# Query stacks of an attention layer filled by twelve moves inside SBUF instead of by a trip over DRAM

## The chip, the cores and the metric

The kernel runs on one core of a Trainium2 chip, with all data in float32. The metric is the time of one execution on the device in microseconds (us). Given are the median, the lowest and the highest of several runs, and one further execution that the hardware profiler recorded.

## The reference

One layer with two residual parts, for 4 sequences of 512 tokens, 1024 wide: attention with 32 query heads of 32 columns that share one head of keys and values, a bias linear in the distance (ALiBi) and a causal mask; then a linear map whose weights are stored as 6-bit codes.

```python
# x: (4, 512, 1024)
h = layernorm(x)
q = (h @ Wq).reshape(b, s, 32, 32)
k, v = split(h @ Wkv)                       # one head of 32 columns each
scores = einsum('bqhd,bkd->bhqk', q, k) * 32**-0.5
scores = where(causal, scores + slopes * (key_pos - query_pos), -inf)
x = x + einsum('bhqk,bkd->bqhd', softmax(scores), v).reshape(b, s, 1024) @ Wo
w = (unpack(qweight) - weight_zero_point) * weight_scale      # (1024, 1024)
x = x + layernorm(x) @ w.T + bias
```

## The kernel before

Every float32 operand of the large products is split into a high and a low part of the fast matmul type (float32r), and a product is the sum of high by high, high by low and low by high. The helper `split` does this: ScalarE rounds to the high part (L412), VectorE subtracts to get the low one (L415).

**Phase one** runs over 4 sequences times 8 groups of 4 heads, so 32 groups. For each group:

- `queries`: 24 matmuls form q transposed in the PSUM tile `pq` (L682: 128 rows = 4 heads x 32 columns, by 512 tokens). `split` writes `qh` and `ql`, each with a single buffer. From them comes the **stack** `qs` of the group, a tile of 126 rows by 4 heads by 512 tokens, in three buffers. Its rows 0 to 31 and 64 to 95 hold qh, rows 32 to 63 hold ql, always with the head's 32 columns as rows and the four heads side by side; rows 96 to 123 hold the bias rows `qr_d`, and two more rows hold the negated row maxima, high and low. As the heads lie below each other in qh and side by side in the stack, the rows have to change partitions. Before, qh and ql are written to the DRAM scratch `q_d` and three moves read them back, rearranged.
- `maxima`: scores `s` against the stack of keys `kst` (L738: 16 matmuls in 10 PSUM banks, of which two are in use at a time), and VectorE takes each row's maximum under the causal mask (L751, into `junk` and `mx`). A transpose on TensorE (`trm`, L767) turns the maxima; their high and low part `mt` go into the stack's last two rows by two small moves (qs<-mt).
- `attention`: scores again, transposed and with the maximum taken off by the stack's rows (`st`, L819, 11 matmuls). ScalarE takes the exponential into `p` (L829), GpSimd masks it (L838) and adds the parts up for the denominators (L860). The products with v (`pav`, L848) and the denominators (`den`, L877) run tiled, four heads next to each other in the array. The result `a` goes to the DRAM scratch `at_d` (L869).

Beside this, phase one prepares the next weights (`wq`, later `wo`; load, ScalarE high part L487, GpSimd low part L489), normalises and turns the tokens of the next sequence (`tr`, L598; `pkv`, L616), and unpacks the codes to the scratch `wf_d` (L912 to L945).

**Phase two** runs over 16 token tiles: load `at_d` and the inverse denominators (`raw`), product with Wo (`po`, L1047), residual, layer norm, transpose, product with the unpacked weights (`pf`, L1167), scale, bias and zero point, store. `ffn_rows` loads the bias, scale and zero-point rows on GpSimd's DMA queue.

All of this is first recorded as operations with a wanted time `at`, a cost, and what each reads and writes. `Work.order` then lays every operation out by estimated costs and due times, in several rounds forwards and backwards, and writes down the order of every engine. So the order on all queues comes from this planner: an operation whose cost or dependences change can move others far away. The planner counts 450 ns on SyncE's queue for issuing one DMA, then its bytes at a shared rate, and 2000 ns until it has landed. All ordinary moves of a kernel run through `move` (L420), so their profile line is L420 whatever they move; SyncE's queue is one queue in order, and a waiting DMA holds up those behind it.

Of the kernel before, what the change touches and what calls it, by code (L numbers as in the profile page):

```python
# [42 lines left out]
P = 128  # L43
# [298 lines left out]
def layer_kernel(  # L342
# [64 lines left out]
    def dma(at, size, fn, out, ins, eng="SP"):  # L407
        work.op(eng, at, 0.0, fn, out, ins, size=size)
# [13 lines left out]

    qr_d = tc.dram_tile([NG, N_BIAS, GH, S], F32R, name="qr_d")
    at_d = tc.dram_tile([NG, P, B * S], F32, name="at_d")
    q_d = tc.dram_tile([4, 2, P, S], F32R, name="q_d")
    rden_d = tc.dram_tile([B, GH, NG, S], F32, name="rden_d")
    qr_i = [work.item() for _ in range(NG)]
    at_i = [work.item() for _ in range(B)]
    q_i = [[work.item() for _ in range(2)] for _ in range(4)]
    rden_i = [work.item() for _ in range(B)]  # L430


# [242 lines left out]
    def queries(at, i):  # L675
        b, g = divmod(i, NG)
        pq = new("ps_q", "q", [P, S], F32, f"pq_{i}")
        hi, lo = wq[g]
        for c in range(KC):
            def three(c=c):  # L680
                for n, (w, s) in enumerate(((hi, 0), (lo, 0), (hi, 1))):
                    nc.tensor.matmul(  # L682
                        pq(), w()[:, c, :], xc[b, c]()[:, s, :],
                        start=(c == 0 and n == 0), stop=(c == KC - 1 and n == 2),
                    )
            h = c // (KC // 2)
# [6 lines left out]
        qs[i] = [(0, GH, new("qs", "qs", [P, GH, S], F32R, f"qs_{i}"))]  # L693
        for s, src in enumerate((qh, ql)):
            dma(
                at + 0.6 + 0.7 * s, 262e3,
                lambda s=s, src=src: move(q_d[i % 4, s], src()), [q_i[i % 4][s]], [src],
            )
        for h, n, q in qs[i]:
            dma(  # L700
                at + 1.0, 57e3 * n,
                lambda h=h, n=n, q=q: move(q()[R_BIAS:R_MAX, :, :], qr_d[g, :, h : h + n, :]),
                [(q, "b")], [qr_i[g]],
            )
# [12 lines left out]
    def part(i, h):  # L717

        return next((q, h - first) for first, n, q in qs[i] if first <= h < first + n)


    S_BANKS = [((3, h),) for h in range(GH)] + [((2, h), (0, h)) for h in range(GH)]
    S_BANKS += [tuple((1, h) for h in (2 * i, 2 * i + 1)) for i in range(2)]
    ROWS = (0, 1, 2, "b")

    def maxima(at, i):
        b = i // NG
        k = kst[b % 2]
        mx = new("small", "mx", [P, GH * NT], F32, f"mx_{i}")
        for n, bank in enumerate(S_BANKS):  # L730
            ps = new("ps_s", "s", [P, S], F32, f"s_{i}_{n}")
            widths = [(t + 1) * P for t, _ in bank]
            places = [sum(widths[:m]) for m in range(len(bank))]

            def products(ps=ps, bank=bank, widths=widths, places=places):
                for (t, h), W, o in zip(bank, widths, places):
                    q, at = part(i, h)
                    nc.tensor.matmul(  # L738
                        ps()[:, o : o + W], q()[0:R_MAX, at, ts(t, P)], k()[0:R_MAX, :W],
                        start=True, stop=True,  # L740
                    )
            pe(
                at + 1.2 * n, widths, products, [ps],
                [(q, r) for q in {part(i, h)[0] for _, h in bank} for r in ROWS] + [k],
                more=5.0,
            )
            for (t, h), W, o in zip(bank, widths, places):
                junk = new("q1", "junk", [P, S], F32, f"junk_{i}_{t}_{h}")
                dve(
                    at + 1.2 * n + 0.3, W,  # L750
                    lambda ps=ps, junk=junk, t=t, h=h, W=W, o=o: nc.vector.tensor_tensor_reduce(  # L751
                        out=junk()[:, :W],
                        in0=ps()[:, o : o + W],
                        in1=mask()[:, S - W :],
                        scale=1.0,
                        scalar=-3e38,
                        op0=ALU.add,
                        op1=ALU.max,
                        accum_out=mx()[:, h * NT + t : h * NT + t + 1],
                    ),  # L760
                    [(mx, (t, h))], [ps], more=125.0,
                )
        at += 1.2 * len(S_BANKS)
        N = GH * NT
        tr = new("ps_misc", "misc", [P, P], F32, f"trm_{i}")
        pe(
            at, [P], lambda: nc.tensor.transpose(tr()[0:N, :], mx(), ident()), [tr], [mx]  # L767
        )
        for s in range(2):
            m = new("mt", f"mt{s}", [N, P], F32R, f"mt{s}_{i}")  # L770
            if s == 0:
                hi = m
                act(at + 0.2, P, lambda: nc.scalar.copy(hi(), tr()[0:N, :]), [hi], [tr])
            else:
                lo = m
                dve(
                    at + 0.4, P,
                    lambda: nc.vector.tensor_tensor(
                        lo(), tr()[0:N, :], hi().bitcast(F32), ALU.subtract
                    ),  # L780
                    [lo], [tr, hi],
                )
            for h, n, q in qs[i]:
                dma(
                    at + 0.5 + 0.2 * s, 2e3 * n,
                    lambda m=m, s=s, h=h, n=n, q=q: move(
                        q()[R_MAX + s : R_MAX + s + 1, :, :], m()[h * NT : (h + n) * NT, :]
                    ),
                    [(q, f"m{s}")], [m],
                )  # L790


    ST_BANKS = [(0, (h,)) for h in range(GH)] + [(1, (h,)) for h in range(GH)]
# [2 lines left out]

    def attention(at, i):
        b, g = divmod(i, NG)
        k = kst[b % 2]
        pr = {}  # L800
        for j in range(NT):
            W = S - j * P
# [2 lines left out]
        for n, (j, heads) in enumerate(ST_BANKS):  # L805
            W = S - j * P
            ps = new("ps_st", "st", [P, len(heads), W], F32, f"st_{i}_{n}")
            own = slice(heads[0], heads[-1] + 1)
            runs = []
            for first, m, q in qs[i]:  # L810
                lo, hi = max(first, heads[0]), min(first + m, heads[-1] + 1)
                if lo < hi:
                    runs.append((
                        q, slice(lo - first, hi - first), slice(lo - heads[0], hi - heads[0])
                    ))

            def products(ps=ps, j=j, runs=runs):
                for q, mine, place in runs:
                    nc.tensor.matmul(  # L819
                        ps()[:, place, :], k()[0:R_ALL, ts(j, P)], q()[0:R_ALL, mine, j * P :],  # L820
                        start=True, stop=True,
                    )
            pe(
                at + 1.2 * n, [len(heads) * W / len(runs)] * len(runs), products, [ps],
                [q for q, _, _ in runs] + [k], more=5.0,
            )
            act(
                at + 1.2 * n + 0.3, len(heads) * W,
                lambda ps=ps, own=own, j=j: nc.scalar.activation(  # L829
                    pr[j]()[:, own, :], ps(), AF.Exp  # L830
                ),
                [(pr[j], h) for h in heads], [ps],
            )
# [466 lines left out]
```

## Time and profile before

| what | value |
|---|---|
| median of 3 runs (lowest to highest) | 829.49 us (828.11 to 829.87) |
| the profiled execution | 825.42 us |
| its span, first to last instruction | 823.5 us |
| granted TensorE clock, mean | 0.994 |
| VectorE, ScalarE, GpSimd busy | 69%, 45%, 62% |
| DMA | 133.39 MB, 162 GB/s on average, 57% of the 16 DMA engines on the main queue |

The profiled execution spends 825.42 - 823.5 = 1.92 us around its span and lies 4.07 us below the median of the runs. Every duration that is taken from the profile belongs to that execution. PE is the TensorE matmul, PEld its weight load, DVE is VectorE, ACT is ScalarE, POOL is GpSimd, SP is SyncE; a q behind the name (SPq) means that engine's sequencer, which issues the DMAs. In the waits, the numbers are the total in us, how many times, and the longest.

### The profile page before, as it was taken

To read this page: it belongs to the slowest core of one execution; us is meant where nothing else is said; L and a number is where in the kernel's file an instruction comes from. 1 tells how busy PE (TensorE), PEld (TensorE's weight loads), DVE (VectorE), ACT (ScalarE), POOL (GpSimd) and SP (SyncE) were. 2 spreads that over 40 slices of the span, in tenths; PEclk is the share of its full clock that TensorE was granted. 3 is DMA by queue.
4 is the path that set the end of the run, shared out by engine and by line. 5 is a ranking of instruction groups with operands and counts; after the bars stand their busy time and mean duration, and the time that the engine had idled before them with its cause. 6 is when DMAs were issued, how large, how long until landed. Compare 5 with 4: busy or idle time off the path is not lost.

```text
span 823.5 us, 13425 instructions
## 1 busy us (share of the span) xinstructions
PE 795.9 (97%) x4480; PEld 594.7 (72%) x4480; DVE 565.5 (69%) x1491; ACT 372.3 (45%) x659; POOL 514.1 (62%) x442
## 2 busy tenths in 40 slices
PE   5979999999999999999999999999999999999997
PEld 4756676777676767676775767667888888888885
DVE  7476777388786388777367675644998666666865
ACT  4336575464775445675556564330233323332320
POOL 4337977276787375877489896879465445554333
PEclk9989999999999999999999999999999999999999
DMA  7885853395553387543567966526875755665321
GB/s 223 245 252 154 232 164 91 111 266 188 155 145 100 106 262 211 148 120 111 174 174 194 235 189 208 170 58 171 214 178 158 173 131 129 152 151 137 97 52 51
DMA packets 131796, 133.39 MB, mean 162 GB/s; under 512 B 42964, under 2 KB 93140, under 8 KB 130704
## 3 DMA queue, kind: packets, MB, share of 16 engines
q1 hardware_dynamic: 130912, 129.01, 57.0%
q0 software_dynamic: 816, 3.53, 1.7%
q8 instruction: 35, 0.57, 0.3%
q14 instruction: 33, 0.27, 0.1%
HBM read 85.58 MB, written 39.85 MB: 152 GB/s over the span
## 4 chain that ended last, share of the span: by engine, by line
PE 89%; DVE 4%; DMA 2%; ACT 2%; issue 1%; POOL 1%; SPq 1%; DVEq 0%; ACTq 0%; POOLq 0%
PE po L1047 21%; PE pq L682 21%; PE pf L1167 13%; PE st L819 9%; PE s L738 9%; PE pav L848 8%; PE den L877 4%; PE pkv L616 2%; PE tr L598 2%; DVE junk L751 2%; ACT p L829 1%; POOL p L860 1%; DMA wo_st<-in_L_attn_Wo_dram 1%; DMA qs<-mt 1%; SPq L420 1%
## 5 line engine op out<-in xcount | busy, mean ns | idle before, releaser
L751 DVE CUSTOM_DVE_ANT_0 junk<-s,mask 128x384 f32<-128x384 f32 (+3 forms) x512 | 250.6, 490 | 119.6 <-PE s L738 88.8
L860 POOL TENSOR_TENSOR p<-p,p 128x1536 f32<-128x1536 f32 (+2 forms) x96 | 232.4, 2421 | 16.7 <-PE pav L848 15.0
L829 ACT ACTIVATE p<-st 128x512 f32<-128x512 f32 (+1 forms) x352 | 183.9, 559 | 115.8 <-PE st L819 110.7
L682 PE MATMUL pq<-xc,wqh 128*128 128x512 f32 x512 | 198.5, 405 | 2.3 <-DVE ql L415 1.4
L1047 PE MATMUL po<-woh,aT 128*128 128x512 f32 x512 | 164.8, 391 | 0.0
L838 POOL TENSOR_SCALAR_AFFINE_SELECT p<-p 128x512 f32<-128x512 f32 x128 | 82.2, 647 | 105.1 <-ACT p L829 104.3
L738 PE MATMUL s<-kst,qs 124*128 124x384 f32 (+3 forms) x512 | 127.5, 324 | 3.9 <-DVE mx L751 3.6
L819 PE MATMUL st<-qs,kst 126*128 126x512 f32 (+1 forms) x352 | 127.1, 399 | 3.9 <-ACT p L829 2.9
L1167 PE MATMUL pf<-wf,xT 128*128 128x512 f32 x512 | 121.1, 390 | 0.7 <-DVE xT L415 0.7
L738 PEld LDWEIGHTS s<-kst,qs 124*128 124x128 f32 x512 | 91.5, 189 | 34.2 <-DVE mx L751 8.9
L682 PEld LDWEIGHTS pq<-xc,wqh 128*128 128x128 f32 x512 | 97.7, 191 | 23.8 <-issue 2.7
L1047 PEld LDWEIGHTS po<-woh,aT 128*128 128x128 f32 x512 | 96.1, 188 | 21.7 <-DVE mx L751 0.8
L1167 PEld LDWEIGHTS pf<-wf,xT 128*128 128x128 f32 x512 | 95.8, 188 | 20.9 <-DVE xT L415 1.1
L682 PE MATMUL pq<-xc,wql 128*128 128x512 f32 x256 | 101.8, 398 | 0.1
L1047 PE MATMUL po<-wol,aT 128*128 128x512 f32 x256 | 99.7, 389 | 0.0
L819 PEld LDWEIGHTS st<-qs,kst 126*128 126x128 f32 x352 | 63.5, 190 | 25.7 <-ACT p L829 10.8
L848 PE MATMUL pav<-p,kv 128*32 128x512 f32 (+3 forms) x1024 | 79.9, 436 | 0.0
L848 PEld LDWEIGHTS pav<-p,kv 128*32 128x32 f32 x1024 | 29.6, 109 | 48.8 <-issue 37.6
L1187 POOL TENSOR_TENSOR x<-x,y 128x512 f32<-128x512 f32 x30 | 42.7, 1425 | 27.4 <-DVE y L1178 27.4
L1047 PEld LDWEIGHTS po<-wol,aT 128*128 128x128 f32 x256 | 48.1, 188 | 9.6
L538 POOL TENSOR_SCALAR rstd_f<-mv_f 128x1 f32<-128x1 f32 x16 | 3.9, 244 | 81.7 <-DVE mv_f L533 72.7
L682 PEld LDWEIGHTS pq<-xc,wql 128*128 128x128 f32 x256 | 49.2, 192 | 7.2 <-POOL wql L489 0.6
(92 smaller groups left out, 878.6 us busy)
## 6 DMA issues: line engine op xcount, KB each, us to landing
qs<-q_d SPq DMA_DIRECT2D x96, 256.0 KB
x<-_attn_hidden_states_dram SPq DMA_DIRECT2D x31, 512.0 KB
q_d<-qh SPq DMA_DIRECT2D x32, 256.0 KB
q_d<-ql SPq DMA_DIRECT2D x32, 256.0 KB
at_d<-a SPq DMA_DIRECT2D x32, 256.0 KB
raw<-at_d SPq DMA_DIRECT2D x16, 512.0 KB
raw<-rden_d SPq DMA_DIRECT2D x64, 128.0 KB
out_dram<-x SPq DMA_DIRECT2D x32, 256.0 KB
```

The lines of the kernel that those rows point to most:

```text
L682: nc.tensor.matmul(pq(), w()[:, c, :], xc[b, c]()[:, s, :], start=(c == 0 and n == 0), stop=(c == KC - 1 and n == 2),)
L738: nc.tensor.matmul(ps()[:, o : o + W], q()[0:R_MAX, at, ts(t, P)], k()[0:R_MAX, :W], start=True, stop=True,)
L751: lambda ps=ps, junk=junk, t=t, h=h, W=W, o=o: nc.vector.tensor_tensor_reduce(out=junk()[:, :W], in0=ps()[:, o : o + W], in1=mask()[:, S - ...
L819: nc.tensor.matmul(ps()[:, place, :], k()[0:R_ALL, ts(j, P)], q()[0:R_ALL, mine, j * P :], start=True, stop=True,)
L829: lambda ps=ps, own=own, j=j: nc.scalar.activation(pr[j]()[:, own, :], ps(), AF.Exp),
L838: nc.gpsimd.affine_select(out=d, in_=d, pattern=[[0, GH], [1, P]], compare_op=ALU.is_ge, fill=0.0, base=0, channel_multiplier=-1,)
L848: nc.tensor.matmul(pav()[ts(h, HD), j * P :], kv[b]()[:, j, HD:], pr[j]()[:, h, :], start=(j == 0), stop=(j == NT - 1), tile_position=(0, ...
L860: nc.gpsimd.tensor_tensor(d, d, pr[j](), ALU.add)
L877: nc.tensor.matmul(d()[ts(h, HD), :], onesel()[:, g, :], pr[0]()[:, h, :], start=(g == 0), stop=(g == NG - 1), tile_position=(0, h * HD),)
L1047: nc.tensor.matmul(po(), aT[s][1]()[:, c, :], w()[:, ts(n, HALF)], start=(c == 0 and m == 0), stop=(c == KC - 1 and m == 2),)
L1167: nc.tensor.matmul(pf(), xT()[:, s, c, :], wf[c]()[:, ts(n, HALF)], start=(c == 0 and s == 0), stop=(c == KC - 1 and s == 1),)
L1187: (nc.vector if last else nc.gpsimd).tensor_tensor(d, d, y(), ALU.add)
```

## The change

The scratch `q_d` and its four copies in turn are gone. Each of the stack's three blocks of 32 rows is now filled by four moves, one per head, straight from `qh` or `ql`: twelve moves of 64 KB in place of two of 256 KB to DRAM and three of 256 KB back. The stack counts as written block by block and head by head, (r, h) in place of r. `qh` and `ql` are in use until all the moves that read them have landed. The parts of the code that allowed a group to have several stacks are gone as well; with one stack per group they did nothing. And the bias and zero-point rows of phase two are wanted 6 us sooner.

```diff
-    q_d = tc.dram_tile([4, 2, P, S], F32R, name="q_d")
-    q_i = [[work.item() for _ in range(2)] for _ in range(4)]
...
-        for s, src in enumerate((qh, ql)):
-            dma(
-                at + 0.6 + 0.7 * s, 262e3,
-                lambda s=s, src=src: move(q_d[i % 4, s], src()), [q_i[i % 4][s]], [src],
-            )
...
-            for r in range(3):
+        q = qs[i] = new("qs", "qs", [P, GH, S], F32R, f"qs_{i}")
+        dma(
+            at + 1.0, 229e3, lambda: move(q()[R_BIAS:R_MAX, :, :], qr_d[g]), [(q, "b")], [qr_i[g]]
+        )
+        for r in range(3):
+            for h in range(GH):
+                src = (qh, ql)[r % 2]
                 dma(
-                    at + 3.0 + 0.1 * r, 65e3 * n,
-                    lambda r=r, h=h, n=n, q=q: move(
-                        q()[ts(r, HD), :, :],
-                        q_d[i % 4, r % 2, h * HD : (h + n) * HD].rearrange(
-                            "(h d) q -> d h q", d=HD
-                        ),
-                    ),
-                    [(q, r)], [q_i[i % 4][r % 2]],
-                )
+                    at + 0.6 + 0.3 * r, 65e3,
+                    lambda r=r, h=h, src=src: move(q()[ts(r, HD), h, :], src()[ts(h, HD), :]),
+                    [(q, (r, h))], [src],
+                )
...
-    ROWS = (0, 1, 2, "b")
+
+    ROWS = [(r, h) for r in range(3) for h in range(GH)] + ["b"]
...
-    ffn_rows(E + 6.0, E + 46.0)
+    ffn_rows(E + 6.0, E + 40.0)
```

More of the change, by code (lines that the diff above doesn't have):

```diff
@@ L691, in queries @@
         split(at, S, qh, ql, pq, qh, ql, pq)
-        qs[i] = [(0, GH, new("qs", "qs", [P, GH, S], F32R, f"qs_{i}"))]
-        for s, src in enumerate((qh, ql)):
-            dma(
-                at + 0.6 + 0.7 * s, 262e3,
-                lambda s=s, src=src: move(q_d[i % 4, s], src()), [q_i[i % 4][s]], [src],
-            )
[L699 to L703, printed above, removed]
-            )
-            for r in range(3):
-                dma(
-                    at + 3.0 + 0.1 * r, 65e3 * n,
-                    lambda r=r, h=h, n=n, q=q: move(
-                        q()[ts(r, HD), :, :],
-                        q_d[i % 4, r % 2, h * HD : (h + n) * HD].rearrange(
-                            "(h d) q -> d h q", d=HD
-                        ),
-                    ),
-                    [(q, r)], [q_i[i % 4][r % 2]],
-                )
-    def part(i, h):
-        return next((q, h - first) for first, n, q in qs[i] if first <= h < first + n)
+        q = qs[i] = new("qs", "qs", [P, GH, S], F32R, f"qs_{i}")
[5 more added lines that the diff above has]
+                src = (qh, ql)[r % 2]
+                dma(
+                    at + 0.6 + 0.3 * r, 65e3,
+                    lambda r=r, h=h, src=src: move(q()[ts(r, HD), h, :], src()[ts(h, HD), :]),
+                    [(q, (r, h))], [src],
+                )
     S_BANKS = [((3, h),) for h in range(GH)] + [((2, h), (0, h)) for h in range(GH)]
     S_BANKS += [tuple((1, h) for h in (2 * i, 2 * i + 1)) for i in range(2)]
-    ROWS = (0, 1, 2, "b")
+    ROWS = [(r, h) for r in range(3) for h in range(GH)] + ["b"]
     def maxima(at, i):
         b = i // NG
-        k = kst[b % 2]
+        k, q = kst[b % 2], qs[i]
         mx = new("small", "mx", [P, GH * NT], F32, f"mx_{i}")
@@ L736, in products @@
                 for (t, h), W, o in zip(bank, widths, places):
-                    q, at = part(i, h)
                     nc.tensor.matmul(
-                        ps()[:, o : o + W], q()[0:R_MAX, at, ts(t, P)], k()[0:R_MAX, :W],
+                        ps()[:, o : o + W], q()[0:R_MAX, h, ts(t, P)], k()[0:R_MAX, :W],
                         start=True, stop=True,
@@ L743, in maxima @@
                 at + 1.2 * n, widths, products, [ps],
-                [(q, r) for q in {part(i, h)[0] for _, h in bank} for r in ROWS] + [k],
+                [(q, r) for r in ROWS] + [k],
                 more=5.0,
@@ L782, in maxima @@
                 )
[L783 to L790, printed above, removed]
+            dma(
+                at + 0.5 + 0.2 * s, 8e3,
+                lambda m=m, s=s: move(q()[R_MAX + s : R_MAX + s + 1, :, :], m()),
+                [(q, f"m{s}")], [m],
+            )
     ST_BANKS = [(0, (h,)) for h in range(GH)] + [(1, (h,)) for h in range(GH)]
@@ L798, in attention @@
         b, g = divmod(i, NG)
-        k = kst[b % 2]
+        k, q = kst[b % 2], qs[i]
         pr = {}
@@ L808, in attention, with products @@
             own = slice(heads[0], heads[-1] + 1)
[L809 to L826, printed above, removed]
+            def products(ps=ps, j=j, own=own):
+                nc.tensor.matmul(
+                    ps(), k()[0:R_ALL, ts(j, P)], q()[0:R_ALL, own, j * P :],
+                    start=True, stop=True,
+                )
+            pe(at + 1.2 * n, [len(heads) * W], products, [ps], [q, k], more=5.0)
             act(
```

## The prediction

> **What bounds the kernel now.** I read the page first: busy time of each engine, the slices, the chain that ended last.
>
> ```profile
> PE 795.9 (97%) x4480; PEld 594.7 (72%) x4480; DVE 565.5 (69%) x1491; ACT 372.3 (45%) x659; POOL 514.1 (62%) x442
> ...
> PE   5979999999999999999999999999999999999997
> ...
> PE 89%; DVE 4%; DMA 2%; ACT 2%; issue 1%; POOL 1%; SPq 1%; DVEq 0%; ACTq 0%; POOLq 0%
> ```
>
> TensorE is busy 97% of the span and is 89% of the chain. One slice of 20.6 us in the middle of the work is weak: the third, 41 to 62 us. The change removes no matmul, so it can only change TensorE's idle time, its turns and its clock. Second, TensorE's waits:
>
> ```profile
> PE s L738 <- DVE mx L751: 3.6, 7, 0.9
> PE st L819 <- ACT p L829: 2.9, 8, 0.5
> ...
> PE st L819 <- DMA qs<-mt: 0.8, 1, 0.8
> ```
>
> No wait for the stack rows (qs<-q_d) is among them. So the trip over DRAM is hidden today, and to shorten it gains nothing directly: what it allows is another order. Third, the weak slice, by windows (after the times: PE busy, PEld, DVE, ACT, POOL, granted clock, DMA share, GB/s) and in the timeline of PE:
>
> ```profile
> 34.60:45.80 11.20, 7.97 (x36) 5.72 (x34) 9.21 (x35) 2.60 (x5) 4.50 (x5) 1.00 1.06 329
> 45.80:49.30 3.50, 3.46 (x8) 2.84 (x9) 3.36 (x9) 0.86 (x2) 1.22 (x4) 0.51 1.11 334
> ```
>
> ```profile
> 34.62 0.63 PE L738 MATMUL s<-kst,qs 124*128 124x512 f32 x2
> ...
> 45.23 0.27 PE L767 MATMUL trm<-ident,mx 128*16 128x128 f32 x1 [1.68 <-DVE mx L751]
> ```
>
> The first group's scores start at 34.62. Their maxima keep DVE busy (9.21 of 11.20 us) while PE has nothing else left, and then the clock stands at 0.51 for 3.5 us. This start-up is the largest loss that the change can touch. Fourth, what a turn into the tiled products (pav, den) costs, from the chain in order of time:
>
> ```profile
> 193.90 0.99 PE den L877 x8
> 194.89 2.15 PE pav L848 x32
> ...
> 210.99 1.64 PE pav L848 x16
> ...
> 218.43 0.79 PE pav L848 x16
> ```
>
> den and both halves of pav in one stretch take 0.99 + 2.15 = 3.14 us; in three stretches 0.99 + 1.64 + 0.79 = 3.42. Each stretch saved is worth (3.42 - 3.14) / 2 = 0.14 us, and some 0.10 more for the last plain product ahead of it, whose spacing grows from 0.23 to about 0.33 us in the trace.
>
> **SyncE's queue.** Per group two writes of q_d and three reads go, twelve direct moves of 64 KB come:
>
> ```profile
> L420 SPq DMA_DIRECT2D qs<-q_d x96: 305/416/1347, 26.6 to 499.0; - x96
> L420 SPq DMA_DIRECT2D q_d<-qh x32: 319/343/1697, 22.4 to 491.9; - x32
> ```
>
> Removed: 2 x 0.343 + 3 x 0.416 = 1.93 us. Added: 12 x 0.343 = 4.12 us (nearest row: a move without rearrangement; bounds 0.305 and 0.416, so 3.7 to 5.0). Net +2.2 us a group. SP spends 194 us issuing in the 529 us from 16 to 545 (the sum of its issue rows there); +32 x 2.2 = 70 makes 264, half the time. The queue has room, but it is in order: behind the twelve moves stand the maxima's rows (qs<-mt), weight loads and stores of a. The qr_d rows now stand before, within or behind them. DMA traffic falls by 32 x 2 x 256 KB = 16.8 MB of 133.4 MB; nobody on PE waits for traffic: 0.
>
> **The path from pq to a full stack.** I read landings from the completion semaphores in the trace (issue to the last update before that semaphore's next use). q_d<-qh: 2.0 us shortest, 2.9 median. qs<-q_d: 3.0 and 4.3. The small qs<-mt: 1.76 and 2.3. Before: eviction 0.6, q_d 0.34 of issue to landing 2.9 in all, two further issues 0.8, landing 4.3: 8.6 us, up to 10 for ql. After: eviction 0.7, then the last of twelve issues starts 11 x 0.343 = 3.8 later, then its landing. No row has a 64 KB move of SP; its landing lies between the 8 KB row's shortest (1.76) and the median of the 256 KB read (4.3). I take 2.5, near the medians of qs<-mt and q_d<-qh, as size hardly counts there. Sum 0.7 + 3.8 + 2.5 = 7.0. With a landing of 4.3, eight semaphores rotate, so the ninth move waits for the first: 0.7 + 4.3 + 3 x 0.34 + 4.3 = 10.3.
> One DMA of about this size does show its landing, on POOL's queue:
>
> ```profile
> kst<-in_k_rows_dram POOLq DMA_DIRECT2D x2, 60.0 KB, 2.9
> ```
>
> With 2.9 the path is 7.4. The Trainium skill (DMA: Bandwidth & Descriptors, Rules for kernel authors) speaks against the change: small transfers should be coalesced, under 64 KB it is mostly overhead. Taken one after the other at that page's fixed 2 us (an estimate), twelve would need 24 us per group and the kernel would be far slower; the four raw<-rden_d of a tile, issued 0.45 us apart and landing after 5.1 us each, show that moves in flight overlap, so I price the issue and one landing.
>
> **What the order gives for it.** The built programs show the order of instructions. I lay PE's order out at the spacings of the trace (0.227 us per 512 columns, tiled stretches as above). Between a group's last pq and its first s stands PE work of 14.4 us (median) before and 11.4 after; counted from the later of pq's end and the release of the stack slot (last st three groups back), after has 9.0 to 12 mostly, the lowest from group 3 on being 7.7, with 5.9 and 8.0 for groups 1 and 2. Against 7.0 to 7.4 all but group 1 have cover. Group 1 falls in the start-up, where DVE's 10 us of maxima lie between, so I put nothing on it. Busy stretches of DMA will exceed 2.5 now and then: 1.5 us lost, bounds 0 and 20 (the second is all groups at 10.3: the sum of the shortfalls from group 3 on).
> qh and ql (one buffer each) are held until twelve landings, not two. ACT's next qh copy waits, behind it the exps and a. From slot release to the next pq's end stand at least 7.4 us of PE work, against 3.8 + 2.5 = 6.3: 0; without that cover, up to 1 us a group, inside the 20.
> PE's wait instructions rise from 153 to 257, 51 ns each in the trace. Hidden or not: 0 to 5.3 us. A matmul with one such wait ahead is late by 5 ns in the median, as the weight load runs ahead; I take 0.5.
>
> **Start-up.** After, the first s stands three pq matmuls before the end of pq1 (before: six matmuls into pq2, which waited 1.45 us for ql). kst is written at 30.2 and stack 0 is full by 22.4 + 3.8 + 2.5, about 29, so s starts at 31.1 instead of 34.6. Then ten s stand in a row: DVE sets the pace, ql of group 1 stands behind six of its banks, near 38.5, and pq2 starts there, not much before. With 18 matmuls of pq2 (at half clock for about 3.4 us, as the row above shows after such gaps) and the last s, group 1's scores start near 45, and 12.4 us of PE work later pq4 near 57.7; before, pq4 starts at 60.7. By then the new order has also done 2.5 us more work: gain 3.0 + 2.5 = 5.5 us. At full clock s of group 1 starts at 42, a gain of 8.7; if the weights of groups 2 and 3, now issued behind twelve moves, come 3 us late, 2.5.
> The row puts the half clock after gaps of 0.9 and 1.7 us. The Trainium skill (TensorE: Matmul & The Clock Gate, The HAM clock gate) has it after an idle window of about 3.4 us; by that the paced s would not halve the clock and the gain would be the 8.7.
>
> **Turns.** Tiled stretches fall from 61 to 47: den and both halves of pav stand together more often. 14 x 0.14 = 2.0 at least, 14 x 0.24 = 3.4 at most; I take 3.0. Scores that come faster than two banks' maxima fall from 12 banks to 6 in the order; most are in the start-up, so 0.5 for the rest.
>
> **Second-phase rows 6 us sooner.** Three DMAs of POOL's queue (bias and zero points, 4.4 and 5.2 us to landing); POOL works 143 of the last 278 us and no PE wait names them. 0; if a bias add (1.24 us) moves into a tile's last sum, 1.3 either way. From 546 us on PE runs po and pf nearly without a gap, so what phase one saves arrives at the end.
>
> **Sum.** -5.5 - 3.0 - 0.5 + 1.5 + 0.5 = -7.0 us. Span 823.5 becomes 816.5, its execution (1.92 us around the span) 825.42 becomes 818.4; the three runs' median is 829.49, 4.07 above that execution, so I forecast 822.5. With the terms at their good ends (8.7 + 3.4 + 0.5 + 1.3) 815.6; at their middling bad ones (2.5 + 2.0, less 3) 828.
>
> **Rivals.** (a) *Stacks come late* (slower). Place: the first s of each group; the price is the gap between path and cover. At a path of 8.5 us the shortfalls sum to 1.7 us, at 9.5 to about 9, which eats the gain; at 10.3 to 20: 829.5 - 9 + 20 = 840 and a half. It decides from a landing of about 3.5 to 4 us. For it: qs<-q_d takes 4.3 today, and PE's order has less cover. Against: that is a DRAM read of four times the size, and traffic falls. Chance 0.20, from 830 to 840.
> (b) *The start gains nothing*: weights and the clock take it back, the turns stay: -3.0 with 0.5 to 1.5 lost, 827 to 828. Chance 0.14.
> (c) *Nothing reaches the end*: the trip was hidden and the new order only moves idle time: 829.5 give or take 1.5. For it: no wait on qs<-q_d. Chance 0.06.
> Main case 0.60, 815 to 828. A measurement can tell about 0.2% (1.7 us) from no change. Faster: 0.60 + 0.10 of (b) + 0.02 of (c) = 0.72; within: 0.04 + 0.04 = 0.08; slower 0.20. The range 814 to 833 takes all of the main case with 1.6 us of room below, (b), (c) and the near part of (a), and leaves out some 0.15.
>
> **What would show it.** Right: first s near 31, pq4 near 58, PE's waits still without qs<-qh or qs<-ql, turn stretches of pav x32 more often, SP's L420 rows at 0.34. Wrong: PE s waiting for DMA qs<-qh or ql in many groups; SP's moves waiting for landings of their own; a half clock in later stretches; gaps in po and pf after 546.

## The result: slower by 3.3%

The changed kernel takes 855.2 us (median of 4 runs, 854.62 to 859.76) where the kernel before takes 828.8 us (4 runs beside it). The ratio is 1.033, 95% interval 1.029 to 1.037. The profiled execution took 854.62 us, its span is 852.7, the mean granted clock 0.985 (before: 825.42, 823.5, 0.994).

From its page: busy time and instructions, PE's and the clock's slices (21.3 us each), traffic, and the chain that ended last:

```profile
PE 800.2 (94%) x4480; PEld 600.6 (70%) x4480; DVE 552.8 (65%) x1491; ACT 370.7 (43%) x659; POOL 520.3 (61%) x442
...
PE   5879798999999999899999898989999999999997
...
PEclk9899999999999999999999999999999999999999
...
DMA packets 127191, 116.66 MB, mean 137 GB/s; under 512 B 46548, under 2 KB 96724, under 8 KB 126096
...
PE 69%; DMA 11%; SPq 9%; DVE 5%; issue 3%; ACT 2%; POOL 1%; DVEq 0%; ACTq 0%; POOLq 0%
```

The weak third slice (7) has become two slices at 7 and two at 8 among the second to the seventh. The instructions are as many as before and 16.7 MB less are moved, but the chain has gone over from PE (89% to 69%) to SyncE's queue and its DMAs (SPq 1% to 9%, DMA 2% to 11%). The stack's moves say what holds that queue; the columns are shortest, median and longest time of one issue in ns:

```profile
L420 SPq DMA_DIRECT2D qs<-qh x256: 507/588/1983, 22.6 to 521.8; - x128
L420 SPq DMA_DIRECT2D qs<-ql x128: 507/588/1673, 25.2 to 524.3; - x128
```

One such issue takes 588 ns, not the 343 of the forecast. The chain in order of time (start, us, what) shows two groups being filled, move by move:

```profile
106.42 0.54 SPq L420
107.00 0.59 SPq L420
107.63 0.59 SPq L420
...
108.95 0.53 SPq L837
...
109.58 4.00 DMA qs<-qr_d
...
113.72 0.47 PE s L720
...
127.07 3.28 DMA qs<-qr_d
130.40 0.50 PE s L720
```

Moves of the stack (L420) start 0.58 to 0.64 us apart; I take 0.635 as the slot (0.588 and some 0.045 between two). L837 is the store of `a`. In this stretch the bias rows qr_d stand behind the twelve, and the scores wait for their landing as well. PE's waits by line (total, times, longest) spread the damage over many names:

```profile
PE st L790 <- ACT p L797: 13.1, 12, 2.3
...
PE st L790 <- DMA qs<-mt: 6.7, 3, 3.0
PE s L720 <- DVE mx L733: 5.6, 8, 1.5
...
PE s L720 <- DMA qs<-qr_d: 2.9, 2, 1.6
```

Before, the first two were 2.9 and 0.8 us. The largest, the wait for ScalarE's `p`, leads back to SyncE's queue as well. ScalarE stands for weights whose loads were issued behind the twelve moves, and `p` stands behind it in its order. Its waits for the Wo weights, after and then before:

```profile
ACT woh L485 <- DMA wo_st<-in_L_attn_Wo_dram: 27.0, 11, 4.4
```

```profile
ACT woh L487 <- DMA wo_st<-in_L_attn_Wo_dram: 11.4, 8, 3.6
```

For the Wq weights they are 20.0 and 8.1 us. One such place in the chain, from the last of twelve moves that began at 501.20:

```profile
508.15 0.59 SPq L420
...
508.84 3.64 DMA wo_st<-in_L_attn_Wo_dram
...
512.50 0.62 ACT woh L485
513.12 0.40 ACT p L797
...
513.57 0.50 PE st L790
```

PE stood there for 1.97 us. Its waits of 2.09 us at 62.18 and of 2.29 at 530.10 lead back to a weight load in the same way, so 6.4 of the 13.1 us are traced to such loads. And the start, PE's timeline:

```profile
30.99 0.63 PE L720 MATMUL s<-kst,qs 124*128 124x512 f32 x2
...
38.13 0.80 PE L680 MATMUL pq<-xc,wqh 128*128 128x512 f32 x1 [0.24 <-DVE ql L415]
...
50.30 0.50 PE L680 MATMUL pq<-xc,wqh 128*128 128x512 f32 x1 [1.89 <-DVE ql L415]
...
62.18 0.67 PE L790 MATMUL st<-qs,kst 126*128 126x512 f32 x1 [2.09 <-ACT p L797]
```

The first scores come 3.6 us sooner, as forecast, and the lead is gone by 62 us. Counting the matmuls done by a given time, the changed kernel is 10 us behind the kernel before at 144 us, 13 at 480, 27 at 560 and 30 at 610; from there on the distance stays. So the loss lies in phase one, above all at its two ends, and at the passage to phase two. Windows of after, then of before (length; busy us and matmuls of PE; then PEld, DVE, ACT, POOL, clock, DMA share, GB/s):

```profile
16.00:145.00 129.00, 113.65 (x627) 82.27 (x627) 84.67 (x272) 67.08 (x125) 76.05 (x71) 0.95 0.58 151
494.00:545.00 51.00, 45.49 (x277) 30.63 (x276) 29.69 (x100) 24.48 (x50) 39.17 (x30) 0.97 0.67 196
```

```profile
16.00:145.00 129.00, 120.83 (x704) 86.61 (x704) 90.12 (x305) 70.21 (x130) 82.45 (x76) 0.97 0.68 187
494.00:545.00 51.00, 50.12 (x314) 35.18 (x314) 29.70 (x81) 23.75 (x49) 35.53 (x31) 1.00 0.53 166
```

### The profile page after: what moved, and what is told of

Same layout as the page of the kernel before. It is cut to its first block, busy times and chain, and to the rows that moved or that the text cites. A ratio compares the mean times of both kernels' runs of the same rounds, so it can differ in the third digit from the quotient of the medians.

```text
span 852.7 us, 13792 instructions
## 1 busy us (share of the span) xinstructions
PE 800.2 (94%) x4480; PEld 600.6 (70%) x4480; DVE 552.8 (65%) x1491; ACT 370.7 (43%) x659; POOL 520.3 (61%) x442
## 2 busy tenths in 40 slices
DMA packets 127191, 116.66 MB, mean 137 GB/s; under 512 B 46548, under 2 KB 96724, under 8 KB 126096
## 4 chain that ended last, share of the span: by engine, by line
PE 69%; DMA 11%; SPq 9%; DVE 5%; issue 3%; ACT 2%; POOL 1%; DVEq 0%; ACTq 0%; POOLq 0%
PE po L1015 18%; PE pq L680 14%; PE pf L1135 12%; SPq L420 7%; PE st L790 7%; PE s L720 7%; PE pav L816 6%; PE den L845 3%; DMA x<-_attn_hidden_states_dram 2%; DVE junk L733 2%; DMA wo_st<-in_L_attn_Wo_dram 2%; DMA qs<-qr_d 2%; PE tr L596 2%; DMA raw<-rden_d 1%; PE pkv L614 1%
## 5 line engine op out<-in xcount | busy, mean ns | idle before, releaser
L680 PE MATMUL pq<-xc,wqh 128*128 128x512 f32 x512 | 203.4, 410 | 2.8 <-DVE ql L415 2.1
L790 PE MATMUL st<-qs,kst 126*128 126x512 f32 (+1 forms) x352 | 130.5, 406 | 19.8 <-ACT p L797 13.1
L720 PE MATMUL s<-kst,qs 124*128 124x384 f32 (+3 forms) x512 | 130.7, 329 | 11.7 <-DVE mx L733 5.6
L720 PEld LDWEIGHTS s<-kst,qs 124*128 124x128 f32 x512 | 94.5, 194 | 40.7 <-DVE mx L733 11.8
L790 PEld LDWEIGHTS st<-qs,kst 126*128 126x128 f32 x352 | 65.5, 194 | 43.0 <-ACT p L797 21.4
L1113 POOL TENSOR_TENSOR x<-x,rows 128x512 f32<-128x512 f32 x32 | 45.0, 1426 | 18.8 <-DVE x L1036 11.9
```

Of the source, the lines that this page charges most:

```text
L680: nc.tensor.matmul(pq(), w()[:, c, :], xc[b, c]()[:, s, :], start=(c == 0 and n == 0), stop=(c == KC - 1 and n == 2),)
L720: nc.tensor.matmul(ps()[:, o : o + W], q()[0:R_MAX, h, ts(t, P)], k()[0:R_MAX, :W], start=True, stop=True,)
L790: nc.tensor.matmul(ps(), k()[0:R_ALL, ts(j, P)], q()[0:R_ALL, own, j * P :], start=True, stop=True,)
L1113: nc.gpsimd.tensor_tensor(d, d, rows["bias"][n][1](), ALU.add)
```

## The experiments

Theory A: the price of an issue. The real slot is 0.635 us and the planner counts 0.450, so its order, made for a queue that is 12 x 0.185 = 2.2 us a group faster than the real one, has SyncE late everywhere. Rivals: B, the new order of PE and the engines beside it, whatever the queue does; C, the second-phase rows that come sooner; D, the direct path itself, which stays dear at any price in the plan. Ratios are to the kernel before, run beside each.

**The rows alone, undone and done** (first edit in the changed kernel, second in the kernel before).

```diff
-    ffn_rows(E + 6.0, E + 40.0)
+    ffn_rows(E + 6.0, E + 46.0)     # e1_rows_late
-    ffn_rows(E + 6.0, E + 46.0)
+    ffn_rows(E + 6.0, E + 40.0)     # e2_rows_early
```

> Changed kernel with the second phase's rows wanted at E+46 again, as before. Theory A (a move inside SBUF holds SyncE's queue 0.59 us, not 0.34, and all behind it comes late): 850 to 860, as the twelve moves are still there. Theory B (the planner's new order is the slower one, whatever the moves cost): also about 855, give or take what a new plan does. Theory C (the rows that come sooner cost the time): back to 829.

Measured: 862.45 us, 1.046 [1.042, 1.049]. Undoing the rows makes the changed kernel slower still (by the ratios 1.2%), so they are not the cause of its loss; with each change of a wanted time the planner makes another order. In this one PE has a wait of 8.7 us at 604 us, `po` for VectorE's `x`, that the changed kernel does not have.

> Kernel before with the rows wanted at E+40 and nothing else changed. A and B: 829, give or take 3. C: towards 855.

Measured: 832.03 us, 1.0068 [1.0046, 1.0089], so a plan with early rows costs 5.6 us, where I had priced that part at nothing. The chain of that run in phase two:

```profile
572.51 6.67 DMA rows<-n_weight_zero_point_dram
579.21 0.69 DVE rows L986
...
585.75 0.64 DVE x L1068
...
586.43 1.09 PE tr L1082 x8
```

VectorE's operation on the rows now stands in its order ahead of a token tile's last normalisation `x`, and waits there until a DMA of GpSimd's queue lands, 6.67 us. PE's transposes `tr` wait for `x`, 2.8 us in all. This chain is only a part of the 5.6 us: counting matmuls as above, that run is level with the kernel before at 480 us, 5 us behind at 545 and 7.6 from 600 on. The changed kernel shows the same chain with 5.48 us for that row and 2.2 us of PE waiting at `tr`; there it is a part of the 3 us that are lost between 560 and 610 us.

**Queue time that the plan does not know, on the old path**: eight further small moves per group, which nobody reads, in the kernel before with its order unchanged.

```diff
-                lambda s=s, src=src: move(q_d[i % 4, s], src()), [q_i[i % 4][s]], [src],
+                lambda s=s, src=src: (move(q_d[i % 4, s], src()), extra(4)),
+                [q_i[i % 4][s]], [src],
+    # extra: nc.sync.dma_start(out=spare()[:, k, :], in_=mask()[0:HD, 0:64])
```

> Kernel before, its order on every engine unchanged, with four extra moves inside SBUF (32 partitions, 256 bytes each, from the mask to a spare tile that nobody reads) behind each of the two writes of q_d: eight a group. If each holds SyncE for 0.59 us as the moves of the changed kernel do, its queue works 194 + 32 x 8 x 0.62 = 353 us in phase one, as in the changed kernel (352). A: 845 to 860. B: 829 to 834, since the order is the old one.

Measured: 901.68 us, 1.091 [1.089, 1.093], far above the 845 to 860 that theory A gave. The added issues take 581 ns in the median although each carries only 8 KB, and PE's largest wait is now for the maxima's rows, which stand behind them:

```profile
PE st L828 <- DMA qs<-mt: 28.1, 13, 4.1
```

So the queue is not roomy: 256 moves of 0.581 + 0.045 = 0.626 us, 160 us of issuing in all, cost 75 us. The reads of `q_d` stand behind the added moves as well, so the path to a full stack is longer too: PE's `s` waits 6.8 us for qs<-q_d, which the kernel before never does. The forecast had taken such time as free as long as the stack was full in time.

**The true price in the plan**: the changed kernel, the planner counting 640 ns for each of the twelve moves, nothing else.

```diff
-                free = s + self.ISSUE[o.eng]
+                free = s + o.issue          # 450 on SP, 640 for the twelve moves
...
-                    [(q, (r, h))], [src],
+                    [(q, (r, h))], [src], issue=640.0,
```

> Changed kernel, but the planner counts 640 ns of SyncE's queue for each of the twelve moves in place of 450. The queue time stays, the plan knows of it. A: part of the loss comes back, 835 to 850. If the whole loss is a plan made with a wrong price: 826 to 832. B in the sense that any order with twelve moves is slow for another reason: 855.

Measured: 827.21 us, 1.0014 [0.9996, 1.0032], 10 runs: the whole loss is gone, with the same moves on the same queue.

```profile
PE st L791 <- DMA qs<-mt: 3.2, 5, 1.2
PE st L791 <- ACT p L798: 2.9, 5, 1.2
PE s L721 <- DVE mx L734: 2.3, 7, 0.6
PE s L721 <- DMA qs<-qh: 1.6, 2, 1.5
```

The wait on ACT's `p` falls from 13.1 to 2.9 us, ScalarE's waits for Wo and Wq weights from 27.0 and 20.0 to 6.5 and 9.7, and SyncE issues as long as in the changed kernel (361 us between 16 and 545 us; 352 in the changed kernel, 194 in the kernel before). Laid out at the spacings of the trace (an estimate), the order now has at least 10.1 us of PE work between the moment a stack can be written and its first scores (from group 3 on); the changed kernel's has 7.7 at least and 9.9 in the median.

**A price half way**, 545 for 640.

> Changed kernel, the planner counts 545 ns for each of the twelve moves, half way between 450 (855 us) and 640 (827 us). If the loss grows with how far the plan's price lies below the queue time: between the two, 834 to 846. If the 28 us were the luck of one plan against another: anywhere from 825 to 860, with no order in it.

Measured: 846.73 us, 1.023 [1.020, 1.025]: between the two, just above the 834 to 846 expected.

**The new order with the old queue**: PE, VectorE, ScalarE and GpSimd run the changed kernel's instructions in its order, but SyncE issues the old two writes and three reads, at the first move of qh, the first of ql and the last of the twelve places.

```diff
+        def stand_in(r, h):
+            left[0] -= 1
+            if r < 2 and h == 0:
+                move(q_d[i % 4, r], (qh, ql)[r]())
+            if not left[0]:
+                # the three reads q()[ts(m, HD)] <- q_d[i % 4, m % 2]
...
-                    lambda r=r, h=h, src=src: move(q()[ts(r, HD), h, :], src()[ts(h, HD), :]),
+                    lambda r=r, h=h: stand_in(r, h),
```

> Changed kernel's order on TensorE, ScalarE, VectorE and GpSimd, unchanged to the last instruction, but on SyncE's queue the moves of the kernel before: the first move of a block writes q_d, the last of the twelve places reads it three times. Queue time per group falls from 12 x 0.63 to about 1.9 us plus a wait of up to 2.5 us for the write. Theory A (queue time that the plan did not know): most of the loss goes, 828 to 838. Theory B (the order itself is slow, with 94 turns in place of 122 and less PE work ahead of each group): stays at 850 to 860.

Measured: 841.89 us, 1.018 [1.015, 1.021], between what theories A (828 to 838) and B (850 to 860) gave. With the engines' order as it is in the changed kernel, a shorter queue alone brings back 12 of the 26 us (841.9 against 827.3 beside it). The rest can't be laid on the order alone, since here a new wait has come in, for the longer trip that begins only at the last place:

```profile
PE s L734 <- DMA qs<-q_d: 12.4, 9, 3.6
```

Counting matmuls as above, this run is 2.5 us behind the kernel before at 480 us, where the changed kernel is 13 behind. Up to there the queue and not the order of the other engines makes the loss. Some 14 us more are lost from there to the end.

**Issue time by itself**: the kernel before, with seven sets of eight moves of several kinds at its end.

```diff
+        eight(lambda k, p, n: nc.sync.dma_start(out=k[p : p + HD, :], in_=m[0:HD, :]))
+        eight(lambda k, p, n: nc.sync.dma_start(out=k[p : p + HD, 0:128], in_=m[0:HD, 0:128]))
+        eight(lambda k, p, n: nc.sync.dma_start(out=at_d[n, 0:HD, 0:S], in_=m[0:HD, :]))
+        eight(lambda k, p, n: nc.sync.dma_start(out=k[p : p + HD, :], in_=at_d[n, 0:HD, 0:S]))
+        ...
```

> Kernel before with seven sets of eight moves at its very end (the bytes go to tiles and a scratch that nobody reads any more), to read each kind's queue time: inside SBUF 32 x 2 KB, 32 x 512 B and 128 x 2 KB; SBUF to DRAM and DRAM to SBUF, 32 and 128 rows of 2 KB. If both ends in SBUF make a move dear: 0.5 to 0.6 us for the first three and 0.33 to 0.42 for the others. If the 32 rows do: 0.5 to 0.6 for all with 32 rows. If the twelve moves were held by the one ahead of them: about 0.34 at every kind's first, more behind it.

Measured in one execution (SyncE's timeline, the second number is a set of eight from first to last; then shortest, median and longest issue in ns for the first set and for the two of 128 rows with an end in DRAM):

```profile
822.69 5.00 SPq L1267 DMA_DIRECT2D kst<-mask  x8
827.73 5.25 SPq L1268 DMA_DIRECT2D kst<-mask  x8
...
841.68 3.87 SPq L1271 DMA_DIRECT2D at_d<-mask  x8
845.60 3.70 SPq L1273 DMA_DIRECT2D kst<-at_d  x8
```

```profile
L1267 SPq DMA_DIRECT2D kst<-mask x8: 528/583/589, 822.7 to 827.2; - x8
L1275 SPq DMA_DIRECT2D at_d<-mask x8: 422/548/649, 849.3 to 853.3; - x8
L1276 SPq DMA_DIRECT2D kst<-at_d x8: 319/320/652, 854.0 to 865.2; - x8
```

Inside SBUF, 32 rows of 2 KB (64 KB) take 528 to 589 ns each, and 32 rows of 512 B as much (512 to 592); eight of the first take 5.00 us, 0.625 apiece. The same 64 KB with one end in DRAM take 0.42 (median 424 ns both ways). So for moves of 32 rows the two ends set the price, not the bytes: my nearest rows had a DRAM end. Moves of 128 rows do not fit that rule. Inside SBUF they took 464 to 527 ns. Written to DRAM, the first four took 422 to 456 and the other four 640 to 649; read back, the first two took 643 and 652 and the other six, each of which had to wait first, 319 or 320. There the moves still in flight seem to count as well, and no run separates that.

**True prices for every odd kind of move**: 640, and also 1330 for the transposing DMAs and 570 for the maxima's rows (issue rows of 1.24 to 1.29 us in the median, and 527 ns); once in the changed kernel, once, without the 640, in the kernel before.

```diff
-                [(q, f"m{s}")], [m],
+                [(q, f"m{s}")], [m], issue=570.0,
...
-            lambda: nc.sync.dma_start_transpose(out=across(), in_=code()), [across], [code],
+            lambda: nc.sync.dma_start_transpose(out=across(), in_=code()), [across], [code],
+            issue=1330.0,      # and so for turned <- halves
```

> Changed kernel, the planner counts the measured queue time of all three kinds of SyncE moves that it has most wrong: 640 ns for the twelve moves, 1330 for a DMA transpose, 570 for a maxima row. If the price of the twelve is the whole story: 827 as with that price alone, give or take 3. If the other two wrong prices cost time too: 815 to 823.

Measured: 845.14 us, 1.022 [1.019, 1.024]. A miss: a truer plan is, by the ratios, some 17 us slower than the one with 640 alone. Its waits are of another kind:

```profile
PE tr L1052 <- DVE x L1038: 7.3, 3, 5.3
PE s L721 <- DVE mx L734: 7.2, 6, 2.5
```

No wait on SyncE's moves is left among the large ones; `tr` is the wait on the early rows, and `mx` follows a VectorE operation that was held up (below).

> Kernel before, the planner counts 1330 ns for a DMA transpose and 570 for a maxima row. The wrong price is 40 transposes x 0.9 us and 64 x 0.1, small against 384 x 0.19 for the twelve moves: 823 to 829. If every wrong price on this queue costs as the twelve do: 815 to 822.

Measured: 828.11 us, 1.0007 [0.9998, 1.0016], 10 runs: nothing on the old path.

**640 with the rows late, and 750**, to see whether 827 is the rule for a plan without a shortfall.

```diff
-    ffn_rows(E + 6.0, E + 40.0)
+    ffn_rows(E + 6.0, E + 46.0)     # e11_true_rows_late, with issue=640.0
+    # e12_price_750: issue=750.0, rows early
```

> Changed kernel with 640 ns counted for each of the twelve moves and the second phase's rows wanted at E+46 again. The run of the kernel before with early rows lost 5.6 us, all near 570 to 590 us, where VectorE waits in order for the zero-point row; with true prices and late rows that loss should go: 820 to 826. If plans with other wishes differ by luck alone: 815 to 850.

Measured: 840.88 us, 1.015 [1.011, 1.019]. Another miss. Its largest PE wait is `s` for `mx`, 9.9 us in 12 places, and one place shows the origin (timelines of VectorE, GpSimd and PE):

```profile
84.56 6.19 DVE L881 TENSOR_SCALAR v<-qw 128x256 int32<-128x256 int32 x1
```

```profile
85.08 2.40 POOL L829 TENSOR_TENSOR p<-p,p 128x1024 f32<-128x1024 f32 x1
87.44 1.25 POOL L488 TENSOR_TENSOR wql<-wq_st,wqh 128x512 fp32r<-128x512 f32 x1
88.66 1.25 POOL L829 TENSOR_TENSOR p<-p,p 128x512 f32<-128x512 f32 x1
```

```profile
91.54 0.51 PE L721 MATMUL s<-kst,qs 124*128 124x256 f32 x2 [4.05 <-DVE mx L734]
```

An unpacking step that takes 0.39 us at its shortest and 0.53 in the median lasts 6.19 beside GpSimd's work, the maxima behind it are late, and PE stands for 4.05 us.

> Changed kernel (early rows), the planner counts 750 ns for each of the twelve moves, above the 635 that they take. If a price below the queue time is what costs: 824 to 835, like 640 and far from 855. If the 827 with 640 was one lucky plan: 840 to 855.

Measured: 843.83 us, 1.019 [1.018, 1.021]. Here too no group is short of cover (by the same estimate 10.3 us at least against a path of 9.7). Enough time for the moves is not sufficient, and the time lies where the expectation put it if the 827 were one lucky plan.

**The same fault on the old path**: the kernel before, its five q_d moves counted at 1 ns each.

```diff
-                lambda s=s, src=src: move(q_d[i % 4, s], src()), [q_i[i % 4][s]], [src],
+                lambda s=s, src=src: move(q_d[i % 4, s], src()), [q_i[i % 4][s]], [src], issue=1.0,
...
-                    [(q, r)], [q_i[i % 4][r % 2]],
+                    [(q, r)], [q_i[i % 4][r % 2]], issue=1.0,
```

> Kernel before with nothing changed but the plan's price of the five q_d moves of a group: 1 ns in place of 450. Really they hold SyncE's queue for 2 x 0.39 + 3 x 0.46 = 2.2 us, so the plan is short by 2.2 us a group; in the changed kernel it is short by 12 x 0.185 = 2.2 us. If such a shortfall is what costs: 840 to 860 with the old data path as well. If the loss belongs to the moves inside SBUF: 826 to 831.

Measured: 836.83 us, 1.011 [1.008, 1.015]. A shortfall of 2 x 0.388 + 3 x 0.461 = 2.2 us a group, as large as the changed kernel's, costs the old path 9 us, not 26, and lies between the two expectations. So the sign of theory A carries over, its size does not.

**How much of it is the luck of one plan?** Three more plans of the direct path at prices near the true one, rows late, and two of the old path at prices beside 450, none with a reason to be better or worse.

```diff
-                    [(q, (r, h))], [src],
+                    [(q, (r, h))], [src], issue=620.0,   # 660.0, 700.0; rows at E + 46.0
```

> Changed kernel, rows wanted at E+46, 620 ns counted for each of the twelve moves (they take 635 with the gap between them). If the direct path costs time even when the plan knows its price: 836 to 846, like 640 (841) and 750 (844). If the planner's luck makes the difference between 827 and 845: spread over 824 to 846.

> The same with 660 ns. Direct path itself: 836 to 846. Luck: 824 to 846.

> The same with 700 ns. Direct path itself: 836 to 846. Luck: 824 to 846.

```diff
-    ISSUE = {"SP": 450, "POOL": 650}
+    ISSUE = {"SP": 470, "POOL": 650}     # and 430
```

> Kernel before, the planner counts 470 ns for every SyncE DMA in place of 450: another plan at about the true price. If a plan's luck is worth 10 us or more whatever the path: anywhere from 820 to 840. If the old path is the less sensitive one: 825 to 830.

> Kernel before, the planner counts 430 ns for every SyncE DMA in place of 450: a third plan of the old path at about the true price. Luck worth 10 us or more on any path: 820 to 840. Old path less sensitive: 825 to 830.

Measured, in this order: 843.64 us, 1.018 [1.014, 1.023]; 842.51, 1.018 [1.015, 1.022]; 834.66, 1.009 [1.006, 1.012]; then 831.49, 1.005 [1.002, 1.007]; 833.45, 1.009 [1.008, 1.012], both above the 825 to 830 of a path that is less sensitive. All plans together, by medians:

| price in the plan | direct path, us | old path, us |
|---|---|---|
| far below the slot | 855.2, 862.5 (450); 846.7 (545) | 836.8 (1 ns) |
| about the slot | 843.6 (620), 827.2, 840.9, 845.1 (640), 842.5 (660), 834.7 (700), 843.8 (750) | 828.8 (450), 828.1 (450 and true others), 833.5 (430), 831.5 (470), 832.0 (450, rows early) |

The seven plans of the direct path at about the right price average 839.7 us, 827 to 845; the five of the old path 830.8, 828 to 834. So the direction that theory A gives holds: every plan with a price well below the slot lies above all those of its path that have it about right, if only just at 545. But 827 was the best of seven, and by these averages the price accounts for some 16 us and something that stays with the direct path (theory D, or the planner's luck with it) for some 9. Two spreads that overlap in one plan do not settle what those 9 us are.

The traces say where the plans part, counting matmuls as above, in one execution each. At 480 us the three plans of the direct path with a price well below the slot are 10 to 13 us behind the kernel before; the seven about the slot lie between 1 ahead and 7 behind, 3 behind on average; the five other plans of the old path, the one at 1 ns among them, lie between 2 ahead and 2 behind. From 480 us to the end, which is the passage to phase two, the three lose another 8 to 22 us, the seven 5 to 19, the five 3 to 9. So up to 480 us the price parts the plans cleanly. Behind it the groups overlap, and there most of the 9 us arise. The cover agrees: with PE's order of each trace laid out as before (an estimate), the shortfalls against a path of 9.7 us sum to some 23, 15 and 7 us for 450 with late rows, 450 and 545, and to less than 2 for each of the seven.

## Why the prediction was wrong, by its own steps

**The step that failed** is "Added: 12 x 0.343 = 4.12 us", with its bounds 0.305 and 0.416. Measured is 0.588 for one issue and some 0.045 behind it, so 12 x 0.635 = 7.6 us a group, outside the bounds. I had taken the row of a move "without rearrangement"; the row that mattered was one of the same kind, inside SBUF with few rows. One stood in the table of before and I used it only for its landing: qs<-mt goes from SBUF to SBUF, and its issue took 514 ns in the kernel before.

With that term the path is 0.7 + 11 x 0.635 + 2.0 = 9.7 us, not 7.0. My landing of 2.5 was too long: from the completion semaphores it is 2.0 in the median. The cover in the order, which I put at 7.7 us at the least, was read rightly. So rival (a) came true in its condition, a path longer than the cover, but by the issue and not by the landing, from which I let it decide. Its sign, PE's `s` waiting for qs<-qh or qs<-ql in many groups, did not come: of `s`, 2.9 us of waits go to the bias rows and 3.2 to no named cause.

**Rival (a) was priced too low as well**, 830 to 840. Its price was PE's wait at the first scores alone. "The queue has room" was the second fault: SyncE issues for 352 us of the 529, not for 264, and what stands behind the twelve moves is late too: the weight loads (ScalarE's waits for them are 19.5 us before and 47.0 after, and at least 6.4 of the 13.1 us of PE's wait for `p` lead back to them), the maxima's rows (0.8 to 6.7 us of waits on PE), and the bias rows, whose landing of 4.0 and 3.3 us is the end of the path in the chain shown above. I named what stands behind the moves and put a price on none of it but the first weights. The added moves on the old path show what this is worth: 75 us for 160 us of issuing, with the old copies and the old order, part of it by the longer way to a full stack.

**The planner's 450** is in the description of the kernel, and I did not hold it against the row for the new kind of move. Where an order is computed from a price, a wrong price costs twice: the move is late, and so is everything that was laid out around it. The price set right brings 26 us back in its best plan and some 16 on average.

**Start-up: half right.** First scores at 30.99 us (forecast 31.1), pq2 at 38.13 (38.5). But the third pq then waits 1.89 us for `ql`, `st` waits 2.09 for ACT's `p` (behind a load of Wq weights), and pq4 comes at 63.92 instead of 57.7, 3 us later than before. The gain of 5.5 did not come.

**The clock.** After the wait of 2.09 us at 62.18 the granted clock is low again (two windows, the columns as above):

```profile
58.92:62.34 3.42, 1.33 (x7) 0.79 (x6) 1.11 (x4) 1.23 (x3) 1.12 (x3) 1.00 0.88 266
62.34:65.75 3.41, 3.41 (x9) 2.59 (x10) 2.54 (x7) 1.96 (x5) 3.30 (x5) 0.50 0.77 234
```

It stands at 0.50 of full speed for 3.41 us, in which PE is busy throughout and does 9 matmuls. The same comes back at 93.06, 349.06, 489.01 and 529.97 us. In the 3.42 us ahead of each of the five, PE is busy for 1.33, 0.50, 1.11, 0.43 and 1.25 us. The sign "a half clock in later stretches" came true; I had priced the half clock in the start-up only, with no repetition. Over the span the share lost is 852.7 x (1 - 0.985) = 12.8 us against 823.5 x (1 - 0.994) = 4.9, so that by this estimate some 8 of the 29 us between the two profiled executions, and not more, are waits paid a second time by the clock. The Trainium skill (TensorE: Matmul & The Clock Gate, What's actually happening) gives an idle window of about 3.4 us. The length of the low stretches agrees. But after the start no wait of PE was as long as that (3.22 us at most): here windows of that length in which PE was partly busy were enough.

**The rows**, priced at "0, 1.3 either way", cost 5.6 us on the old path, in a plan that differs elsewhere too. I asked whether PE waits for them, but not who waits in VectorE's order behind the operation that does.

**Right:** traffic (133.39 to 116.66 MB; forecast 16.8 less), the turns into tiled products (61 to 47) and that the first stack is full by 31 us. The turns' 3.0 us and the price of PE's wait instructions no run separates. The rule of the Trainium skill that I cited (DMA: Bandwidth & Descriptors, Rules for kernel authors: coalesce small transfers) gave the right sign. The cause in these runs was not the fixed time of a transfer, since landings overlap and take 2.0 us, but the issuing queue.

**Left open:** which part of the 9 us that remain at the right price belongs to the direct path's busier queue, and which to the planner's draw. Most of these 9 us arise behind 480 us. VectorE's late maxima weigh more in these plans (`s` waiting for `mx`: 6.1, 7.2, 9.9, 11.2, 5.3 and 4.7 us at 620, 640 with all prices true, 640 with the rows late, 660, 700 and 750; 3.6 before, 5.6 in the changed kernel, but only 2.3 in the best), and no run isolates why.

## What to carry to other kernels

Price a new DMA by a row of the same kind, the same two ends and the same number of rows, not by one of about the same size: here the wrong row gave a forecast gain of 7 us where a loss of 26 was measured. A queue that issues in order is a resource with its own budget, and what stands behind the added moves has to be priced like the path itself. Where a planner makes the order, give it the measured slot of every new operation first, and compare several plans by small shifts of a constant before a difference of one per cent is credited to the change: here such shifts moved the old path by 5 us and the new one by 18. No plan of the direct path was faster than the kernel before.

## What the runs showed of the hardware that was not expected

- An issue on SyncE's queue of 32 rows inside SBUF takes some 585 ns, whether the rows have 2 KB (583 to 588 in the median), 512 B (588) or, in the added moves, 256 B (581); 465 for most moves of 128 rows inside SBUF; 424 for 32 rows to or from DRAM. Fewer rows inside SBUF cost more than 128. For 128 rows with an end in DRAM the same kind of move took between 319 and 652 ns.
- PE's granted clock halved for 3.41 us in five places of the changed kernel, each time after a window of that length in which PE was busy for 0.43 to 1.33 us and no single wait was longer than 3.22 us.
- A VectorE step on int32 data that takes 0.39 us at its shortest took 6.19 beside GpSimd's uninterrupted work (5.36 in another plan; the longest of such steps in the kernel before took 3.70). The Trainium skill (SBUF — State Buffer, SBUF: two separate sides) has the two engines share a port pair that one instruction holds whole while the other blocks, for VectorE operations in a two-port mode or with two inputs in SBUF. Whether this step is one of them no run shows. The 6.19 us agree with a blocking of that sort, but go over several GpSimd instructions in a row, and GpSimd's own (2.40, 1.25, 1.25 us) keep their pace. Which of the two gives way was not tried.
